# Cross-attention energies on one Trainium2 core: three products in one PSUM bank, scaled in place

## The chip, the cores and the metric

The kernel runs on one core of one Trainium2 chip. The metric is the device time of one execution in microseconds, as the median of several runs. A core has five engines that matter here: TensorE (matrix products into PSUM; its weight loads have a row of their own in the profile, PEld), VectorE (DVE), ScalarE (ACT), GpSimd (POOL) and SyncE (SP), which issues DMAs. PSUM is the memory that TensorE writes: 128 partitions by 8 banks, a bank being 512 float32 values in each partition.

## The reference

There are 32 batches, each with a query input `y` and a key/value input `x` of 256 channels by 1024 positions.

```
x_q = einsum('oc,bcn->bno', w_qk, y)
x_k = einsum('oc,bcn->bon', w_qk, x)
x_v = einsum('oc,bcn->bon', w_v, x) + b_v
energy    = einsum('bnc,bcm->bnm', x_q, x_k)          # 1024 x 1024 a batch
attention = softmax(energy, axis=-1)
attention = attention / (1e-07 + attention.sum(axis=1, keepdims=True))
x_r = einsum('bcn,bnm->bcm', x_v, attention)
x_r = relu(einsum('oc,bcn->bon', w_t, x - x_r) + b_t)
return x + x_r
```

The softmax goes along a row of the energies; the second division goes by the column sums of the softmax.

## The kernel before

**Folding and splitting.** The two query/key weights are folded into one matrix, so the energies are `y` transposed times `G x`. `y` and `G x` are each split into a high part, a low part and a scaled high part (`Split.parts` on ScalarE, then the accumulating DMAs `lower` and `mixed` on GpSimd's queue), and the energies of a block of 128 rows are the sum of three products of such parts, called forms 0, 1 and 2 here. The tiles are `yf` and `gf`. All other large products use a seven-product scheme for 2 x 2 blocks: the class `Seven`, with `Keys` (g, prints as `pg`), `Values` (u, prints as `pu`) and `Attention` (o, prints as `po`). Its methods p1 to p7 are the products, c11 to c22 the combinations. Each uses three PSUM banks, `one`, `two` and `three`: p1, p6, p7 and p4 share `one`, p5 and p3 share `two`, and p2 has `three`.

**Energies.** A batch has 8 blocks `n` of 128 rows. `Energy.products(h)` does one half (512 columns) of a block: six matmuls, forms 0 and 1 into one bank and form 2 into another. `gather(h)` then has ScalarE scale the first bank by `-OVER` into an SBUF tile `es`, and VectorE add the second bank to it, write the result into `e` and take the row minimum (`nm`, carried from half 0 to half 1). `exp` runs on ScalarE over the 1024 columns of `e` in place, with the minimum as its bias, and collects the row sum `rs`. `share` is VectorE's: the reciprocal `ri` of the row sum and `acc += e * ri`, the running column sums. In the loop, `exp` of block n-1 and `share` of block n-2 are issued with block n.

**After the last block** the order of the work is: g.p1, g.p5, `exp(7)`, `share(6)`, g.p2, c11, `share(7)`, g.p6, `columns`, g.p3, c12, g.p7, c22, then the products of `Values` for the next batch, then `inverse` (the reciprocal column sums, `rc`), then the splits for the next batch between the other work, then `Attention`. In `Attention.run` VectorE multiplies `e` by `ri` and `rc` in pieces (`normal`), forms sums of quarters in `et` (`mix`), and TensorE follows with `xpart` and `epart`.

g.p1 and g.p5 are each followed by a ScalarE copy out of PSUM (`gp1s`, `gp5s`), and g.p6 by the copy `gw`; g.p7 accumulates into the bank that `gw` reads.

**Order and buffers.** The wrapper `InOrder` puts the operations of each engine into the order in which the program calls them, so an engine's queue is exactly the order of the source. Every engine operation goes through that wrapper, which is why all of them have line 73 in the profile. PSUM is one pool of eight banks that are handed out in turn: `bank(name)` takes the next one that is free.

The last batch is different: it has no next batch to prepare, and it keeps the unfinished banks of the batch before it (`before`) open while its own energies run.

Of the kernel before, what the change touches and what calls it, by code (L numbers as in the profile page):

```python
# [9 lines left out]
F32 = mybir.dt.float32  # L10
F32R = mybir.dt.float32r
AF = mybir.ActivationFunctionType
ALU = mybir.AluOpType
AX = mybir.AxisListType
# [3 lines left out]
def kernel(  # L18
# [23 lines left out]
    B, C, N = x.shape  # L42
    P = 128
    KC = C // P
    NT = N // P
    MB = 512
    MH = N // MB
# [5 lines left out]
    BIG = 3.0e38  # L53
    UP = 4096.0
    UNDER = 1.0 - 2.0**-13
    OVER = 1.0 + 2.0**-12

    const = ctx.enter_context(tc.tile_pool(name="const", bufs=1))
    xp = ctx.enter_context(tc.tile_pool(name="xp", bufs=2))
    ps_m = ctx.enter_context(tc.tile_pool(name="ps_m", bufs=8, space=bass.MemoryType.PSUM))  # L60

    class InOrder:


        def __init__(self, engine):
            self.engine = engine
            self.last = None
# [9 lines left out]

    pe, dve, act, pool = (InOrder(g) for g in (nc.tensor, nc.vector, nc.scalar, nc.gpsimd))

    def bank(name):  # L80
        return ps_m.tile([P, MB], F32, tag="m", name=name)

    loaded = {}

# [50 lines left out]
    behind = const.tile([P, 1], F32, name="behind")  # L135
    parts = const.tile([P, NB, NG + 1], F32, name="parts")
    dve.memset(parts[:, :, NG], EPS)
    idle = bank("idle")
    for _ in range(5):
        pe.matmul(idle[:, :P], few, few, start=True, stop=True)  # L140
    make_identity(nc, ident)
# [19 lines left out]
        return w, (a11, a12, s4, a22, s1, s2, s3)  # L161


    pg = [bank(f"pg_{i}") for i in range(KC)]
    for i in range(KC):
        for k in range(KC):
            pe.matmul(
# [2 lines left out]
    _, g_left = lefts("g", pg, UP)  # L170

    def turned_weights():

        pt = [bank(f"pt_{i}") for i in range(KC)]
        for i in range(KC):
            for k in range(KC):
                pe.transpose(pt[i][:, ts(k, P)], wt[:, k, ts(i, P)], ident)
        return lefts("wtT", pt)

    def value_weights(wtT):  # L180

        pw = [bank(f"pw_{i}") for i in range(KC)]
        for i in range(KC):
            for k in range(KC):
                pe.matmul(
                    pw[i][:, :C], wv[:, k, ts(i, P)], wtT[:, k, :], start=(k == 0), stop=(k == KC - 1)
                )
        return lefts("wvtT", pw, -1.0)[1]

    def value_bias(wtT):  # L190

        pb = bank("pb")
        for k in range(KC):
            dve.tensor_scalar(bvs[:, k], few, bv[:, k], None, ALU.add)
        for k in range(KC):
            pe.matmul(pb[:, :C], bvs[:, k], wtT[:, k, :], start=(k == 0), stop=(k == KC - 1))
        act.mul(bu.rearrange("p k c -> p (k c)"), pb[:, :C], -1.0)
        act.mul(nbt[:, :, 0], bt[:, :, 0], -1.0)
# [5 lines left out]
    sp = ctx.enter_context(tc.tile_pool(name="sp", bufs=4))  # L204

    def temp(tag, name):
        return cp.tile([P, MB], F32, tag=tag, name=name)
# [67 lines left out]
    class Seven:  # L275
# [3 lines left out]
        def __init__(self, name, b):  # L279
            self.name = name  # L280
            self.b = b

        def bank(self, j):
            return bank(f"p{self.name}{j}_{self.b}")

        def kept(self, p, tag):
            s = temp(tag, f"{self.name}{tag}_{self.b}")
# [107 lines left out]
    class Energy:  # L395
# [3 lines left out]
        def __init__(self, b, n, yf, gf):  # L399
            self.b, self.n = b, n  # L400
            self.yf, self.gf = yf, gf
            self.low = BIG

        def products(self, h):
            self.sums = [bank(f"pe{j}_{self.b}_{self.n}_{h}") for j in range(2)]
            for j in range(3):
                for k in range(KC):
                    pe.matmul(
                        self.sums[j // 2],
                        self.yf[:, j, k, ts(self.n, P)],  # L410
                        self.gf[:, j, k, ts(h, MB)],
                        start=(k == 0 and j != 1),
                        stop=(k == KC - 1 and j != 0),
                    )

        def gather(self, h):


            s = temp(("p1s", "p5s")[h], f"es_{self.b}_{self.n}_{h}")
            act.mul(s, self.sums[0], -OVER)  # L420
            nm = sp.tile([P, 1], F32, tag=f"nm{h}", name=f"nm_{self.b}_{self.n}_{h}")
            dve.tensor_tensor_reduce(
                out=e[:, self.n, ts(h, MB)],
                in0=self.sums[1],
                in1=s,
                scale=1.0,
                scalar=self.low,
                op0=ALU.add,
                op1=ALU.min,
                accum_out=nm,  # L430
            )
            self.low = nm

        def exp(self):
            self.rs = sp.tile([P, 1], F32, tag="rs", name=f"rs_{self.b}_{self.n}")
            row = e[:, self.n, :]
            act.activation(row, row, AF.Exp, bias=self.low, scale=-1.0, accum_out=self.rs)

        def share(self):

# [160 lines left out]
    def columns(b):  # L601

        dve.tensor_reduce(
            parts[:, :, 0],
            acc.rearrange("p (j r) -> p j r", r=G32),
            AX.X,
            ALU.add,
            apply_transpose=True,
        )
# [26 lines left out]
    xr, _ = summed(0)  # L636
    g = Keys(0, xr)
# [26 lines left out]
    u = Values(0, xr)  # L664
# [11 lines left out]
    for b in range(B):  # L676
        more = b + 1 < B
        rows = []

        for n in range(NT):  # L680
            now = Energy(b, n, q.to, g.split.to)
            rows.append(now)
            now.products(0)
            if n == 0:
                e = ep.tile([P, NT, N], F32, tag="e", name=f"e_{b}")
                acc = one.tile([P, N], F32, tag="acc", name=f"acc_{b}")
            now.gather(0)
            now.products(1)
            now.gather(1)
            if n == 0:  # L690
                if b == 0:
                    u.p4()
                    u.c21()
                    xsteps[1]()
                    xsteps[2]()
                elif more:
                    load(b + 1)
                if b == 0:
                    ur, usteps = u.factors()
                    for step in usteps:  # L700
                        step()
                if more and b > 0:
                    xn, xsteps = summed(b + 1)
            if n > 0:
                rows[n - 1].exp()
            if n > 1:
                rows[n - 2].share()
            if more and b > 0 and n in (2, 4, 6):
                xsteps[n // 2 - 1]()

        if more:
            q = Queries(b + 1)
            for i in range(KC):
                q.load(i, nc.sync.dma_start)
            g = Keys(b + 1, xn)
            g.p1()
            g.p5()
            rows[-1].exp()
            rows[-2].share()
            g.p2()  # L720
            g.c11()
            rows[-1].share()
            g.p6()
            columns(b)
            g.p3()
            g.c12()
            g.p7()
            g.c22()
            un = Values(b + 1, xn)
            un.p1()  # L730
            un.p5()
            un.p2()
            un.p6()
        else:
            before.xpart(before.one, 7, True)
            rows[-1].exp()
            rows[-2].share()
            before.epart(before.one, 7)
            ur, usteps = u.factors()
            now = Attention(b, xr, ur)  # L740
            now.begin()
            rows[-1].share()
            columns(b)
            for step in usteps:
                step()
            before.p7s = temp("w", "p7s")
            act.copy(before.p7s, before.one)
        rc = inverse(b)
        if more:
            q.parts(0)  # L750
            q.lower(0)
            un.p3()
            g.p4()
            g.c21()
            un.p7()
            q.parts(1)
            q.lower(1)
            q.mixed(0)
            g.split.parts(0)
            q.mixed(1)  # L760
            g.split.lower(0)

            def between():
                g.split.parts(1)
                g.split.lower(1)
                g.split.mixed(0)
                g.split.mixed(1)

            now = Attention(b, xr, ur)
            now.begin()  # L770
            now.run(un, between=between)
            pool.tensor_copy(behind, now.t4[:, HT - 1, :1])
            if b + 2 < B:
                now.close()
                ur, usteps = un.factors()
                for step in usteps:
                    step()
            else:
                now.epart(now.two, 3, (3,))
                now.c12()  # L780
                now.put()
            before = now
            xr, u = xn, un
        else:
            before.end()
            now.run(None, before)
            now.finish()
# [30 lines left out]
```

## Time and profile before

| | |
|---|---|
| median of 3 runs | 2130.79 us (2130.71 to 2130.84) |
| the profiled execution | 2130.66 us, span 2128.9 us |
| mean granted TensorE clock | 0.994 |
| TensorE busy | 2087.1 us, 98% |
| VectorE busy | 1812.7 us, 85% |
| ScalarE busy | 1179.7 us, 55% |
| GpSimd busy | 681.3 us, 32% |

The span is the time from the first to the last instruction; about 1.8 us of the execution lie around it. Matmuls are pipelined and their ends are modelled, so a busy TensorE is not TensorE at its peak. In the rows, `out<-in` names the tiles that an operation writes and reads (`e<-pe,es` is the operation of `gather` on VectorE), and `x` at the end is a count. A number in brackets is the idle time of the engine before the row, with what released it. A batch in the steady part takes 65.03 us (573.44 to 638.47 us is one). The groups that the change touches:

| operation, before | count | mean |
|---|---|---|
| energy matmul, 128x512 (`pe`) | 3072 | busy 718.7 us in all |
| ScalarE scaling, 128x512 (`es<-pe`) | 512 | 595 ns |
| VectorE add and minimum, half 0 (`e<-pe,es`) | 256 | 686 ns |
| VectorE add and minimum, half 1 (`e<-pe,es,nm`) | 256 | 751 ns |
| VectorE accumulator read (`nm`) | 512 | 83 ns |
| ScalarE exponential, 128x1024 (`e<-e,nm`) | 256 | 1143 ns |
| VectorE `acc`, 128x1024 | 224 | 1294 ns |

### The profile page before, as it was taken

The page shows a single profiled execution, that of the slowest core. Times are in us where ns is not written, and L with a number is a line of the kernel's source. Part 1 is how long each engine was busy: PE and PEld are TensorE (multiplying, and loading weights), DVE is VectorE, ACT ScalarE, POOL GpSimd, SP SyncE. Part 2 cuts the span into 40 slices and gives each one's busy share as a digit, 9 for nine tenths or more (in the row PEclk, how much of TensorE's full clock was granted, in tenths as well). Part 3 has the DMA queues.
Part 4 walks back from the last instruction along what each step waited for, and adds up shares of the span by engine and source line. Part 5 has one row for each costly group of instructions (what it writes and reads, how often), then busy time and mean ns, then how long its engine had stood idle before and what let it go on. Part 6 is the DMA issues. An engine that isn't in the chain of part 4 may idle for free.

```text
span 2128.9 us, 23494 instructions
## 1 busy us (share of the span) xinstructions
PE 2087.1 (98%) x7586; PEld 1290.6 (61%) x7586; DVE 1812.7 (85%) x3024; ACT 1179.7 (55%) x1802; POOL 681.3 (32%) x582
## 2 busy tenths in 40 slices
PE   5999999999999999999999999999999999999998
PEld 4666556665556665566655566655666555666564
DVE  1988889888899888898888998888888889988898
ACT  3664556655556645566555566455665555664562
POOL 2333331333332333323333323333233333233321
PEclk7999999999999999999999999999999999999999
DMA  8456766557766567665577665676655776656740
GB/s 206 88 127 163 177 154 129 139 136 181 168 128 145 129 163 178 155 133 134 136 179 167 128 146 128 163 178 150 135 138 135 177 170 127 148 127 162 178 95 30
DMA packets 108954, 310.34 MB, mean 146 GB/s; under 512 B 10784, under 2 KB 11552, under 8 KB 108832
## 3 DMA queue, kind: packets, MB, share of 16 engines
q0 software_dynamic: 58192, 174.87, 44.9%
q1 hardware_dynamic: 50496, 133.85, 18.5%
q8 instruction: 60, 0.98, 0.2%
q14 instruction: 62, 0.51, 0.1%
q10 hardware_dynamic: 144, 0.13, 0.0%
HBM read 124.78 MB, written 33.55 MB: 74 GB/s over the span
## 4 chain that ended last, share of the span: by engine, by line
PE 61%; DVE 29%; issue 4%; ACT 1%; DMA 1%; DVEq 0%; POOL 0%; ACTq 0%; POOLq 0%
PE pe L73 31%; PE po L73 28%; DVE e L73 14%; DVE acc L73 4%; DVE et L73 4%; DVE gfr L73 3%; DVE rc L73 2%; DVE sc L73 1%; PE pu L73 1%; DVE parts L73 1%; ACT es L73 1%; DVE ri L73 0%; DMA gf<-gfr 0%; PE pg L73 0%; DMA gf<-gf 0%
## 5 line engine op out<-in xcount | busy, mean ns | idle before, releaser
L73 PE MATMUL pe<-gf,yf 128*128 128x512 f32 x3072 | 718.7, 394 | 10.9 <-DMA gf<-gf 10.9
L73 PEld LDWEIGHTS pe<-gf,yf 128*128 128x128 f32 x3072 | 578.0, 188 | 145.7 <-issue 27.3
L73 ACT ACTIVATE es<-pe 128x512 f32<-128x512 f32 x512 | 304.2, 595 | 184.7 <-PE pe L73 184.4
L73 PE MATMUL po<-et,us 128*128 128x512 f32 x768 | 353.9, 597 | 11.5 <-DVE et L73 11.5
L73 DVE SCALAR_TENSOR_TENSOR e<-e,ri,rc 128x512 f32<-128x512 f32 x512 | 347.4, 746 | 1.1
L73 DVE SCALAR_TENSOR_TENSOR acc<-e,ri,acc 128x1024 f32<-128x1024 f32 x224 | 289.9, 1294 | 8.0
L73 ACT ACTIVATE e<-e,nm 128x1024 f32<-128x1024 f32 x256 | 292.7, 1143 | 3.4 <-DVE nm L73 3.3
L73 PEld LDWEIGHTS po<-et,us 128*128 128x128 f32 x768 | 142.9, 190 | 207.0 <-issue 158.4
L73 DVE CUSTOM_DVE_ANT_0 e<-pe,es,nm 128x512 f32<-128x512 f32 x256 | 192.2, 751 | 76.5 <-ACT es L73 49.4
L73 PE MATMUL po<-e,ut 128*128 128x512 f32 x512 | 225.0, 592 | 1.0 <-DVE e L73 1.0
L73 POOL DMA_DIRECT2D yf<-yfr x64 | 55.0, 860 | 533.0 <-ACT yf L73 518.6
L73 DVE CUSTOM_DVE_ANT_0 e<-pe,es 128x512 f32<-128x512 f32 x256 | 175.5, 686 | 51.6 <-ACT es L73 39.1
L73 ACT ACTIVATE z<-po,bt 128x512 f32<-128x512 f32 x31 | 21.4, 689 | 337.1 <-DMA out_dram<-z 234.5
L73 PEld LDWEIGHTS po<-e,ut 128*128 128x128 f32 x512 | 97.2, 190 | 123.8 <-issue 107.4
L73 DVE TENSOR_TENSOR et<-e 128x1024 f32<-128x1024 f32 x128 | 153.7, 1221 | 4.4
L73 POOL TENSOR_TENSOR ut<-ut,bu 128x1024 f32<-128x1024 f32 x64 | 153.5, 2473 | 0.0
L73 POOL DMA_DIRECT2D gf<-gf x64 | 54.8, 856 | 306.3 <-DMA gf<-gfr 262.8
L73 DVE SCALAR_TENSOR_TENSOR z<-z,x 128x512 f32<-128x512 f32 x96 | 132.2, 1377 | 3.3
L73 ACT ACTIVATE yf<-yf 128x1024 fp32r<-128x1024 f32 x128 | 128.2, 1049 | 2.0
L73 ACT ACTIVATE gf<-gf 128x1024 fp32r<-128x1024 f32 x128 | 128.2, 1049 | 2.0
L73 PE MATMUL po<-e,us 128*128 128x512 f32 x256 | 125.3, 592 | 0.0
L73 POOL DMA_DIRECT2D xs<-xs x31 | 37.2, 1201 | 248.4 <-DMA xs<-in_x_dram 240.9
(106 smaller groups left out, 2753.7 us busy)
## 6 DMA issues: line engine op xcount, KB each, us to landing
yfr<-in_ctx_dram SPq DMA_DIRECT2D x64, 512.0 KB, 5.8
yf<-yfr POOLq DMA_DIRECT2D x64, 512.0 KB, 5.1
gf<-gfr POOLq DMA_DIRECT2D x64, 512.0 KB, 10.6
yf<-yf POOLq DMA_DIRECT2D x64, 512.0 KB, 8.0
gf<-gf POOLq DMA_DIRECT2D x64, 512.0 KB, 5.2
out_dram<-z SPq DMA_DIRECT2D x128, 256.0 KB, 3.5
x<-in_x_dram SPq DMA_DIRECT2D x31, 1024.0 KB, 7.4
xs<-in_x_dram SPq DMA_DIRECT2D x62, 512.0 KB, 5.1
```

Of the source, the lines that this page charges most:

```text
L73: self.last = getattr(self.engine, name)(*args, **kwargs)
```

## The change

The two halves of a block now lie in a pair of neighbouring banks, one bank a half. `first()` runs forms 0 and 1 of both halves into the pair, and ScalarE scales the pair in place, 1024 columns in one operation from PSUM to PSUM. `second()` runs form 2 of both halves on top of the scaled values, and VectorE takes one row minimum over the pair. `exp` reads the pair in PSUM and writes `e`. The SBUF tiles `es`, the add on VectorE and the second minimum are gone.

The order is one step deeper: with block n are issued `second` of block n-1, `exp` of block n-2 and `share` of block n-3. What is left over after the last block moves behind it: `exp(6)`, `share(5)` and `second(7)` stand between g.p1 and g.p5.

The banks are no longer handed out in turn. PSUM is one tile of eight banks, and everything has a fixed place: block n of a batch takes pair n mod 4 (n mod 3 in the last batch, banks 0 to 5), g takes banks 2, 0 and 1 as `one`, `two`, `three`, u takes 3, 4, 5, and o takes 6, 7, 0 (7, 4, 5 in the last batch).

```diff
-    ps_m = ctx.enter_context(tc.tile_pool(name="ps_m", bufs=8, space=bass.MemoryType.PSUM))
+    ps_m = ctx.enter_context(tc.tile_pool(name="ps_m", bufs=1, space=bass.MemoryType.PSUM))
...
-    def bank(name):
-        return ps_m.tile([P, MB], F32, tag="m", name=name)
+    banks = ps_m.tile([P, 8, MB], F32, name="banks")
+
+    def bank(j):
+        return banks[:, j]
...
+            last = name == "o" and b == B - 1
+            self.places = {"g": (2, 0, 1), "u": (3, 4, 5), "o": (7, 4, 5) if last else (6, 7, 0)}[name]
 
         def bank(self, j):
-            return bank(f"p{self.name}{j}_{self.b}")
+            return bank(self.places[(1, 5, 2).index(j)])
...
-            self.low = BIG
-
-        def products(self, h):
-            self.sums = [bank(f"pe{j}_{self.b}_{self.n}_{h}") for j in range(2)]
-            for j in range(3):
-                for k in range(KC):
-                    pe.matmul(
-                        self.sums[j // 2],
-                        self.yf[:, j, k, ts(self.n, P)],
-                        self.gf[:, j, k, ts(h, MB)],
-                        start=(k == 0 and j != 1),
-                        stop=(k == KC - 1 and j != 0),
-                    )
-
-        def gather(self, h):
...
+            at = 2 * (n % (4 if b + 1 < B else 3))
+            self.pair = banks[:, at : at + 2]
+
+        def products(self, forms):
+            for h in range(MH):
+                for j in forms:
+                    for k in range(KC):
+                        pe.matmul(
+                            self.pair[:, h],
+                            self.yf[:, j, k, ts(self.n, P)],
+                            self.gf[:, j, k, ts(h, MB)],
+                            start=(j == 0 and k == 0),
+                            stop=(j == 2 and k == KC - 1),
+                            skip_group_check=True,
+                        )
+
+        def first(self):
+
+            self.products((0, 1))
+            act.mul(self.pair, self.pair, -OVER)
+
+        def second(self):
+
+            self.products((2,))
+            self.low = sp.tile([P, 1], F32, tag="nm", name=f"nm_{self.b}_{self.n}")
+            dve.tensor_reduce(self.low, self.pair.rearrange("p h m -> p (h m)"), AX.X, ALU.min)
 
         def exp(self):
             self.rs = sp.tile([P, 1], F32, tag="rs", name=f"rs_{self.b}_{self.n}")
-            row = e[:, self.n, :]
-            act.activation(row, row, AF.Exp, bias=self.low, scale=-1.0, accum_out=self.rs)
+            act.activation(
+                e[:, self.n, :],
+                self.pair.rearrange("p h m -> p (h m)"),
+                AF.Exp,
+                bias=self.low,
+                scale=-1.0,
+                accum_out=self.rs,
+            )
...
-            now.products(0)
+            now.first()
...
-            now.gather(0)
-            now.products(1)
-            now.gather(1)
+            if n > 0:
+                rows[n - 1].second()
...
-            if n > 0:
-                rows[n - 1].exp()
             if n > 1:
-                rows[n - 2].share()
+                rows[n - 2].exp()
+            if n > 2:
+                rows[n - 3].share()
...
             g = Keys(b + 1, xn)
             g.p1()
+            rows[-2].exp()
+            rows[-3].share()
+            rows[-1].second()
             g.p5()
             rows[-1].exp()
             rows[-2].share()
...
         else:
+            rows[-2].exp()
+            rows[-3].share()
+            rows[-1].second()
             before.xpart(before.one, 7, True)
             rows[-1].exp()
             rows[-2].share()
```

More of the change, by code (lines that the diff above doesn't have):

```diff
@@ L137 @@
     dve.memset(parts[:, :, NG], EPS)
-    idle = bank("idle")
+    idle = bank(7)
     for _ in range(5):
@@ L161, in lefts @@
         return w, (a11, a12, s4, a22, s1, s2, s3)
-    pg = [bank(f"pg_{i}") for i in range(KC)]
+    pg = [bank(i) for i in range(KC)]
     for i in range(KC):
@@ L172, in turned_weights @@
     def turned_weights():
-        pt = [bank(f"pt_{i}") for i in range(KC)]
+        pt = [bank(6 + i) for i in range(KC)]
         for i in range(KC):
@@ L180, in value_weights @@
     def value_weights(wtT):
-        pw = [bank(f"pw_{i}") for i in range(KC)]
+        pw = [bank(4 + i) for i in range(KC)]
         for i in range(KC):
@@ L190, in value_bias @@
     def value_bias(wtT):
-        pb = bank("pb")
+        pb = bank(6)
         for k in range(KC):
@@ L416, in gather @@
-        def gather(self, h):
[L419 to L432, printed above, removed]
+            at = 2 * (n % (4 if b + 1 < B else 3))
```

## The prediction

> **What bounds the kernel now.** I read the page first, then the chain of waits from 568 to 640 us (one whole batch in the steady part), then the timelines of the engines there. The page says that TensorE is nearly always busy and that the chain is shared:
>
> ```profile
> PE 2087.1 (98%) x7586; PEld 1290.6 (61%) x7586; DVE 1812.7 (85%) x3024; ACT 1179.7 (55%) x1802; POOL 681.3 (32%) x582
> ...
> PE 61%; DVE 29%; issue 4%; ACT 1%; DMA 1%; DVEq 0%; POOL 0%; ACTq 0%; POOLq 0%
> ```
>
> In one batch the chain runs on TensorE through attention and energies, crosses to VectorE near the last energies, and comes back after the normalisation:
>
> ```profile
> 573.44 21.36 PE pe L73 x94
> ...
> 595.52 0.68 DVE e L73
> ...
> 600.64 1.30 DVE acc L73
> ...
> 607.50 6.73 DVE e L73 x10
> ...
> 616.90 1.24 DVE et L73
> 618.13 0.04 issue
> 618.18 2.84 PE po L73 x6
> ```
>
> So a batch (65.03 us from 573.44 to 638.47) is decided in two places: when VectorE gets through its queue, and when TensorE gets to the products that use `et`. The weight loads show how near TensorE is at the second place (gap of an unhindered load: 0.24):
>
> ```profile
> 616.83 0.19 PEld L73 LDWEIGHTS po<-et,us 128*128 128x128 f32 x1 [0.24 <-issue]
> 618.18 0.30 PEld L73 LDWEIGHTS po<-et,us 128*128 128x128 f32 x2 [1.16 <-DVE et L73]
> ...
> 619.57 0.19 PEld L73 LDWEIGHTS po<-xs,wtTs 128*128 128x128 f32 x1 [0.24 <-issue]
> ```
>
> Loads come 0.43 apart, so five after 616.83 would be at 618.98; it is 619.57. TensorE has only 0.59 us to spare in the whole stretch. Any TensorE delay between the energies and 616 beyond 0.59 lengthens the batch. That is what I look for.
>
> **Durations.** ScalarE's timeline gives the blocks' pace and the end of the energies:
>
> ```profile
> 591.07 0.59 ACT L73 ACTIVATE es<-pe 128x512 f32<-128x512 f32 x1
> ...
> 593.79 0.59 ACT L73 ACTIVATE es<-pe 128x512 f32<-128x512 f32 x1
> 594.88 0.60 ACT L73 ACTIVATE es<-pe 128x512 f32<-128x512 f32 x1 [0.50 <-PE pe L73]
> ...
> 597.47 1.15 ACT L73 ACTIVATE e<-e,nm 128x1024 f32<-128x1024 f32 x1
> ...
> 598.71 0.59 ACT L73 COPY gw<-pg 128x512 f32<-128x512 f32 x1
> ```
>
> One block is 2.72 us of TensorE, 0.2267 a matmul. The first `pg` matmul is at 595.08; the matmul before the `es` of 594.88 is two from the end and ends at 594.63, so a reader starts 0.25 after its matmul. VectorE meanwhile needs 2.94 a block (its pairs of `e<-pe,es` start at 586.70, 589.64, 592.58, 595.52): it is the slower one and falls 0.86 behind.
>
> **Part 1, VectorE per block.** Removed: the two `e<-pe,es` with their accumulator reads, 1.55 us (586.70 to the reciprocal at 588.25). Added: one minimum over 1024 elements of PSUM, which the trace does not have. Rows: a 512-wide TENSOR_TENSOR from PSUM is 0.68 and the next starts 0.60 after it; 512 more elements cost 0.54 (SBUF TENSOR_TENSOR 1.22 at 1024, 0.68 at 512). So 1.22 to its result, 1.14 to the next start. Bounds: small TENSOR_REDUCE rows (32x160 in 0.307, 32x32 in 0.175 to 0.203) give 0.81 to 1.03 ns an element, 1.01 us at the least; twice the 512 row is 1.36. I take 1.14, by the nearest row in source and width. With the share (reciprocal and `acc`, 597.06 to 598.45: 1.39) a block needs 2.53, less than TensorE's 2.72: VectorE keeps up and its backlog goes. Who is late next? The order.
>
> **Part 2, the end of the energies.** Everything is one block deeper: after TensorE's last block there now wait `share(4)`, `share(5)`, the last reduction, `share(6)`, c11, `share(7)`, where before there were `share(5)`, `share(6)`, c11, `share(7)`. TensorE finishes all but the last four energy matmuls at 595.08 - 0.91 = 594.17. Then VectorE: reduction 6 from 594.42, `share(4)` from 595.56, `share(5)` from 596.95, reduction 7 from 598.34, result 599.56. The last exponential starts at 599.62; before, 597.47: 2.15 later. ScalarE's queue is in order, and behind that exponential stands the copy `gw` that g.p7 on TensorE needs (1.24 after the exponential, load another 0.63 later, from 598.71 and 599.34). So g.p7 moves from 599.34 to 601.49, and all of TensorE's work behind it, x parts and epart(one, 1) too: +2.15. Less the spare 0.59: **+1.56 a batch**. VectorE's own way is shorter: `share(6)` 599.48, c11 600.87, `share(7)` 601.47 against 600.45, +1.02, so `et` is there at 619.15 when TensorE arrives at 619.41.
>
> The other moved steps have cover. `second(7)` stands behind g.p1 on TensorE, with its four matmuls (0.91) ahead of g.p5; its result is in PSUM by 597.9, and VectorE is not free for it before 598.34. `exp(6)` stands on ScalarE behind `gp1s` and is done by 598.7; `share(6)` asks for it at 599.48. `exp(7)` ends, with its accumulator, at 600.86; `share(7)` asks at 601.47.
>
> A second wait lies under the first one. g.p1 now writes bank 2, which exponential 5 reads. Forms 0 and 1 of the last block end at 593.27, their scaling (0.595 plus 0.43 for 512 more: 1.02) starts at 593.52, the exponential at 594.45, done 595.6: TensorE waits there from 593.94 to 595.64, 1.7 us, with the last energies queued behind. Alone it would bring g.p7 to 600.64, +1.30, or +0.71 a batch. It holds even if the reduction were free.
>
> **Part 3, at no cost.** Scaling 128x1024 in PSUM: bounds 0.98 (512 row plus 0.38) to 1.19 (two rows); with the exponential (1.24 to the next start) about 2.2 us of ScalarE a block, under 2.72, covered by TensorE's 2.72; above it, each 0.1 us costs 0.8 a batch. The exponential from PSUM: 0.69 for 512 with a bias plus 0.43, 1.12, like the 1.14 now; bounds 1.05 to 1.38. TensorE's 12 matmuls a block stay 12. ScalarE's splits and GpSimd's DMAs for the next batch slip by 2.15 while the energies slip by 1.56; the third form is first needed in `second(0)`, 2.7 us later than now, which covers it. SP's loads wait for nothing new.
>
> **Part 4, the two ends.** First batch: TensorE waits for the third form's DMAs:
>
> ```profile
> 41.55 0.77 PE L73 MATMUL pe<-gf,yf 128*128 128x512 f32 x1 [4.49 <-DMA gf<-gf]
> 47.76 3.32 PE L73 MATMUL pe<-gf,yf 128*128 128x512 f32 x7 [5.44 <-DMA gf<-gf]
> ```
>
> Forms 0 and 1 of block 1 and the product u.p4 can now go ahead of that wait, 12 matmuls and 8 small ones, so the energies end 4.0 us earlier (67.8 for 71.8). The deeper tail, with the first three `acc` at 1.8 to 2.5 us as they are there now, lets reduction 7 end at 74.1 and g.p7 start at 76.0 instead of 78.34; with the spare there (0.98 by the loads) **-3.3**, between -6 and 0. Last batch: three pairs, so a block waits for the exponential three before it, which stands behind the newest scaling: 1.81 for eight matmuls, 0.25 to wake ScalarE, 0.93 and 1.14 there, 0.2 to wake TensorE, 4.33 a block from block 3 on, not 2.72. Counted from the first energy matmul: block 3 begins at 8.9, block 7 at 26.2; reduction 6 at 29.15, reduction 7 at 33.1 behind two shares, its exponential until 35.7, `share(7)` until 37.2, and 0.8 for the slow last `acc` (2.10) that is there now too. `columns` starts at 38.0 instead of 30.1 (2060.1 to 2090.22): **+7.9**, bounds 5 and 10.
>
> **Sum.** The profiled execution is 2130.66 (span 2128.9 and 1.8 around it), 0.13 under the median. 30 batches x 1.56 = 46.8; 2130.66 + 46.8 - 3.3 + 7.9 = 2182. With the reduction between 1.01 and 1.36 and some tenths of wake-up time, +1.1 to +2.2 a batch: 33 to 66. Ends: 2130.7 + 33 - 6 + 5 = 2163 and 2130.7 + 66 + 0 + 10 = 2207.
>
> The new pauses of TensorE (1.7 and 0.7 us a batch) raise one question. Behind the pauses of 4.49 and 5.44 us in the first batch, the seven matmuls of the row above take 0.47 us each, twice the usual; behind the 0.9 us wait at 618.18 they do not slow down. For 1.7 us no row of before decides, and I take the nearer one, no slowing. [...]
>
> **Rivals.** (a) Faster: VectorE's backlog is all that matters. Its place is 595.52, where it is 0.86 behind; taken away in 31 batches, with the ends, 2130.7 - 26.7 + 7.9 = 2112. For it: the chain does pass there, and VectorE loses 0.41 a block. Against: it decides only if the last exponential starts before 598.06 (597.47 + 0.59) and g.p1 does not wait, which needs a reduction of 0.36 us, under every row. 5%. (b) Pauses slow TensorE: seven matmuls at 0.47 instead of 0.23 are 1.7 us, once a batch: 2182 + 51 = 2233. 6%. (c) ScalarE becomes the bound: if operations in PSUM cost a quarter more than my rows, 2.72 is passed; at 2.9 a block 31 x 8 x 0.18 = 45 more, 2227. 4%. (d) The change does not do what it says: `banks` is one tile, and if waits are made for the whole tile instead of for banks, scaling and reductions stop TensorE in every block, about 2 us x 256 = 500, 2640. 2%. (e) The waits cancel, within 4 us of now. 3%.
>
> **How the numbers follow.** The forecast gets 80%. A difference under 0.2% (4.3 us) can't be told from no change. Faster: (a) and a little of the rest, 0.06. Same: 0.03. Slower: forecast, (b), (c), (d), 0.91. The range is the forecast's 2163 to 2207, widened slightly for wake-up times I can't see: 2158 to 2208.
>
> **What would show it.** Right: in the chain, `gw` or the last exponential between VectorE and `pg`; a TensorE wait of about 1.7 us at the first `pg` load and another before g.p7; no `et` wait at the later products; reductions of 1.2 us; a batch of 66.6 us; 4.3 us between blocks in the last batch. Wrong: a steady batch under 65 us, blocks further apart than 2.72 in the middle, or matmuls of 0.47 after the pauses.

## The result, and the profile after the change

The changed kernel takes 2182.99 us (median of 5 runs, 2182.50 to 2184.16) against 2130.71 us (median of 5 runs now, three of them those of the table above): a ratio of 1.0247, 95% interval 1.0232 to 1.0262. The forecast was 2182, slower. The profiled execution is 2182.99 us with a span of 2181.2, 52.3 more than before.

The page of the changed kernel, shares of the engines and of the chain:

```profile
PE 2097.1 (96%) x7586; PEld 1291.8 (59%) x7586; DVE 1764.8 (81%) x2256; ACT 1155.4 (53%) x1546; POOL 682.2 (31%) x582
...
PE 86%; DVE 9%; ACT 3%; DMA 1%; issue 1%; DVEq 0%; ACTq 0%; POOLq 0%
```

VectorE and ScalarE have less to do than before (VectorE by 48 us), and the kernel is slower all the same. VectorE's share of the chain fell from 29% to 9%: it no longer carries the path through the normalisation, but only one short stretch a batch. The chain of waits shows that stretch (in all rows after the change, every PSUM tile is called `banks`):

```profile
604.77 1.22 DVE nm L73
...
606.10 1.29 DVE acc L73
...
607.50 1.28 DVE acc L73
608.78 1.14 DVE nm L73
...
610.01 1.21 ACT e L73 x2
611.22 0.48 ACT gw L73
611.70 0.04 issue
611.74 59.41 PE banks L73 x222
```

Reduction 6, two shares, reduction 7, the last exponential, the copy `gw`, and then TensorE for 59.41 us until the same place in the next batch. TensorE's weight loads show both waits at the end of the energies (an unhindered load has 0.24 in the brackets):

```profile
606.03 0.30 PEld L73 LDWEIGHTS banks<-x,g 128*128 128x128 f32 x2 [1.79 <-ACT e L73]
...
611.74 0.30 PEld L73 LDWEIGHTS banks<-xs,gs 128*128 128x128 f32 x2 [1.06 <-ACT gw L73]
...
629.66 0.19 PEld L73 LDWEIGHTS banks<-et,us 128*128 128x128 f32 x1 [0.24 <-DVE et L73]
```

The first is g.p1 at its bank, the second g.p7 behind `gw`. The third is the fifth of the eight loads of `et`, the one that waited 1.16 us before: TensorE now comes too late to wait there. From one `gw` to the next a batch takes 66.50 us, before 65.03.

### The profile page after: what moved, and what is told of

It reads as the page before. It is cut to its first block, busy times and chain, and to the rows that moved or that the text cites. A ratio compares the mean times of both kernels' runs of the same rounds, so it can differ in the third digit from the quotient of the medians.

```text
span 2181.2 us, 21835 instructions
## 1 busy us (share of the span) xinstructions
PE 2097.1 (96%) x7586; PEld 1291.8 (59%) x7586; DVE 1764.8 (81%) x2256; ACT 1155.4 (53%) x1546; POOL 682.2 (31%) x582
## 4 chain that ended last, share of the span: by engine, by line
PE 86%; DVE 9%; ACT 3%; DMA 1%; issue 1%; DVEq 0%; ACTq 0%; POOLq 0%
PE banks L73 86%; DVE acc L73 4%; DVE nm L73 4%; ACT e L73 2%; ACT gw L73 1%; DMA gf<-gf 0%; DVE ri L73 0%; DVE e L73 0%; DMA gf<-gfr 0%; ACT banks L73 0%; ACT yf L73 0%; ACT gf L73 0%; DVE et L73 0%; DVE parts L73 0%; DVE rc L73 0%
## 5 line engine op out<-in xcount | busy, mean ns | idle before, releaser
L73 PE MATMUL banks<-gf,yf 128*128 128x512 f32 x3072 | 740.4, 400 | 13.0 <-ACT e L73 6.7
L73 PEld LDWEIGHTS banks<-gf,yf 128*128 128x128 f32 x3072 | 578.8, 189 | 163.5 <-issue 37.3
L73 DVE TENSOR_REDUCE nm<-banks 128x1 f32<-128x1024 f32 x256 | 313.1, 1223 | 213.8 <-PE banks L73 204.2
L73 ACT ACTIVATE banks<-banks 128x1024 f32<-128x1024 f32 x256 | 258.1, 1008 | 223.7 <-PE banks L73 223.6
L73 PE MATMUL banks<-et,us 128*128 128x512 f32 x768 | 345.6, 592 | 0.8 <-DVE et L73 0.8
L73 ACT ACTIVATE e<-banks,nm 128x1024 f32<-128x1024 f32 x256 | 284.7, 1112 | 20.0 <-DVE ri L73 16.4
L73 PEld LDWEIGHTS banks<-et,us 128*128 128x128 f32 x768 | 145.8, 190 | 185.1 <-issue 176.1
L73 PE MATMUL banks<-e,ut 128*128 128x512 f32 x512 | 225.0, 592 | 1.6 <-DVE e L73 1.6
L73 PE MATMUL banks<-e,us 128*128 128x512 f32 x256 | 125.3, 592 | 0.0
L73 PE MATMUL banks<-et,ut 128*128 128x512 f32 x256 | 115.1, 592 | 0.0
```

What stands on the lines that cost most here:

```text
L73: self.last = getattr(self.engine, name)(*args, **kwargs)
```

## The experiments

The batch times in this section go from one `gw` copy to the next on ScalarE's timeline. Each experiment's ratio is to the kernel before, run again beside it (2130.37 us for e1 to e4, 2131.14 us for e5 to e8). The last two columns say where two steps stand in a steady batch (the one that runs at 600 us), counted from its first energy matmul: the weight load of g.p7 on TensorE, and the start of `share(7)` on VectorE.

| kernel | median, us | ratio to the kernel before (95%) | a batch in the steady part, us | g.p7 | `share(7)` |
|---|---|---|---|---|---|
| before | 2130.71 | 1 | 65.03 | 26.46 | 27.57 |
| changed | 2182.99 | 1.0247 (1.0232 to 1.0262) | 66.50 | 28.54 | 28.62 |
| e1: g in other banks | 2190.83 | 1.0284 (1.0270 to 1.0298) | 66.50, five of 68.1 to 68.4 | 28.53 | 28.61 |
| e2: `gw` ahead of the last exponential | 2187.28 | 1.0267 (1.0253 to 1.0281) | 66.63 | 28.08 | 29.16 |
| e3: both | 2168.57 | 1.0179 (1.0165 to 1.0193) | 66.04 | 26.48 | 28.60 |
| e4: last batch, exponential first | 2175.18 | 1.0210 (1.0196 to 1.0224) | 66.47 | 28.50 | 28.58 |
| e5: another order throughout | 2116.90 | 0.9933 (0.9920 to 0.9945) | 64.67 | 27.51, behind u.p1 | 26.61 |
| e6: e5 without the filled wait | 2128.59 | 0.9989 (0.9980 to 0.9998) | 65.03 | 27.08 | 26.62 |
| e7: e1 with the wait filled | 2170.62 | 1.0184 (1.0170 to 1.0198) | 66.07 | 28.53, behind u.p1 | 28.61 |
| e8: kernel before, one share later | 2166.63 | 1.0165 (1.0151 to 1.0179) | 66.20 | 26.46 | 28.74 |

### e1 to e3: which of the waits decides

e1 gives g banks that are free early; e2 changes ScalarE's order; e3 does both.

```diff
-            self.places = {"g": (2, 0, 1), "u": (3, 4, 5), "o": (7, 4, 5) if last else (6, 7, 0)}[name]
+            self.places = {"g": (0, 1, 2), "u": (3, 4, 5), "o": (7, 4, 5) if last else (6, 7, 1)}[name]
```

> Only the fixed places of g and o change (g: banks 0, 1, 2 instead of 2, 0, 1; o: 6, 7, 1 instead of 6, 7, 0), so g.p1 no longer writes a bank that exponential 5 reads. Theory (the order on ScalarE: g.p7 waits for gw behind the last exponential behind reduction 7): the 1.8 us wait at the first g load goes, but g.p7 stays where it is, about 28.5 us after the first energy matmul of its batch, because reduction 7 waits for VectorE's shares and not for TensorE; 2183 us, within 4. Rival (the bank wait is what costs): the batch loses 0.7 us, 30 x 0.7 = 21, 2162 us.

```diff
             g.p5()
-            rows[-1].exp()
             rows[-2].share()
             g.p2()
             g.c11()
-            rows[-1].share()
             g.p6()
+            rows[-1].exp()
+            rows[-1].share()
             columns(b)
```

> Only the place of the last exponential changes: ScalarE takes gw (after g.p6) first and exponential 7 behind it. Theory: gw then waits for g.p6 on TensorE, which the bank wait still holds until about 610.5 on the clock of the changed kernel's batch, so g.p7 comes only 0.4 us earlier; exponential 7 moves 1.2 us later and share(7) 0.7 us later; VectorE becomes what ends last, 1.75 us behind the kernel before, a batch of 66.8 us, 30 x 0.3 = 9 us more than the changed kernel: 2192 us. Rival (only the TensorE wait at g.p7 counts): 30 x 0.4 = 11 us less, 2172 us.

> Both edits together: g in banks 0, 1, 2 and gw ahead of the last exponential. Theory: TensorE goes through g without a wait, and what is left is VectorE's deeper queue, 1.05 us a batch behind the kernel before; the wait for et at the later products comes back. Batch 66.1 us, 30 x 0.4 = 12 us under the changed kernel: 2171 us. Rival (the two TensorE waits are the whole cost): a batch of 65.0 us as before, 2183 - 44 = 2139 us. Rival (the bank wait is what costs): no more than from the bank change alone.

Measured: in e1 the wait at the first g load is gone, g.p7 stays where it was (28.53 us, the theory's 28.5), and a batch is still 66.50 us. So the bank wait costs nothing as long as `gw` comes late: the rival of 2162 us falls. But the time was 2190.8, 4 us above the theory's bound. Five slower batches make that up: together they lose 8.45 us, and the profiled execution of 2191.1 us would be 2182.7 without it. What slowed them is taken up under e7.

In e2 g.p7 comes 0.46 us earlier and the batch is longer, 66.63 us, because the last exponential now holds up `share(7)` by 0.54 us; the chain crosses to VectorE there and returns to TensorE at `et`, as it did in the kernel before. The theory had a batch of 66.8 and 9 us more than the changed kernel, the rival under 66.2 and 11 us less; measured are 4.3 us more.

In e3 g.p7 is back at 26.48, `share(7)` is still at 28.60, and the batch is 66.04 us, the theory's 66.1. The weight loads of e3 show the old wait again, longer than before the change:

```profile
624.84 0.30 PEld L73 LDWEIGHTS banks<-et,us 128*128 128x128 f32 x2 [1.36 <-DVE et L73]
```

So without TensorE's two waits, VectorE's deeper queue alone costs 1.0 us a batch. TensorE's waits and VectorE's queue are two paths of nearly one length, and taking one away leaves the other.

### e4: the last batch

```diff
+            if not more and n > 1:
+                rows[n - 2].exp()
             now.first()
...
-            if n > 1:
+            if more and n > 1:
                 rows[n - 2].exp()
```

> Only the last batch changes: ScalarE takes exponential n-2 ahead of the scaling of block n, not behind it. Theory (with three pairs, a block waits for the exponential three before it, which stands behind the newest scaling): blocks come 2.7 to 2.9 us apart instead of 4.38, five blocks x 1.5 = 7 to 8 us less, 2175 us. Rival (the last batch loses its 8 us in the deeper tail, whatever the pairs): 0 to 2 us less.

Measured: 2175.2 us, 7.8 less than the changed kernel; the steady batches are the same to 0.03 us. TensorE's timeline of the last batch, first in the changed kernel (two of five such blocks), then in e4:

```profile
2117.55 3.02 PE L73 MATMUL banks<-gf,yf 128*128 128x512 f32 x12 [1.35 <-ACT e L73]
2121.93 3.04 PE L73 MATMUL banks<-gf,yf 128*128 128x512 f32 x12 [1.36 <-ACT e L73]
```

```profile
2104.59 22.08 PE L73 MATMUL banks<-gf,yf 128*128 128x512 f32 x92
```

The blocks came 4.38 us apart with three pairs of banks, and come with no gap in the row once the exponential that frees a pair does not stand behind a scaling that has time. Three pairs are enough; the queue order was the price.

### e7: what slowed e1

TensorE reaches g.p7 earlier in e1 and then waits for `gw` in one piece (2.68 us idle between weight loads). In five of its batches (the expectation below counts six) the products behind that wait are slower. TensorE's timeline of e1, the product u.p1 in a batch of 66.5 us, and the same place in one of 68.4, with the pause ahead of it:

```profile
613.62 1.05 PE L73 MATMUL banks<-wvtT,x 128*128 128x128 f32 x8
```

```profile
1412.69 1.12 PE L73 MATMUL banks<-xs,gs 128*128 128x512 f32 x2 [1.86 <-ACT gw L73]
1413.65 1.57 PE L73 MATMUL banks<-wvtT,x 128*128 128x128 f32 x8
1415.02 1.91 PE L73 MATMUL banks<-wvtTs,xs 128*128 128x128 f32 x8
```

The granted clock from 1411 to 1416 is 0.80, against 1.00 in the 4 us before. The copy `uw`, which follows u.p6, starts 6.98 to 7.02 us after `gw` in each of the five slow batches and 5.36 or 5.37 us after it in the others from the third on. To tell the pause from the places of the banks, e7 keeps the places and puts u.p1 into the pause:

```diff
             g.c12()
+            un = Values(b + 1, xn)
+            un.p1()
             g.p7()
             g.c22()
-            un = Values(b + 1, xn)
-            un.p1()
             un.p5()
```

> The bank change of e1 and u.p1 ahead of g.p7, nothing else. Theory (e1's six batches of 68.1 us come from a lower TensorE clock after the pause before g.p7, which is 2 us long there): the pause is 1.1 us, no batch is slowed, TensorE's delay falls under VectorE's, and the batch is VectorE's 66.1 us: 2171 us. Rival (those batches are slowed by the places of the banks): several batches stay 1.6 us longer than the others.

Measured: 2170.6 us, batches of 66.07 us, and from the third on none over 66.4. In e1's rows the pause is 1.85 us idle at 612.66, and the next product starts 0.90 after u.p1 (613.62 to 614.52), so an estimate of what is left of the pause here is 0.95. `uw` starts 4.46 or 4.47 us after `gw` from the third batch on; in the second, of 67.25 us, it is 6.11. The places, kept from e1, are not the cause: with the pause shortened, no later batch is slowed.

### e8: depth alone, in the kernel before

```diff
-            if n > 1:
-                rows[n - 2].share()
+            if n > 2:
+                rows[n - 3].share()
...
+            rows[-3].share()
             g.p1()
             g.p5()
```

The same line stands ahead of the last batch's tail.

> The kernel before, with its two banks a half and its SBUF scaling, where only share is one block later (share(n-3) in the loop, one more share behind the last block). Theory (depth of the order costs, not the place of the energies): VectorE ends its shares 1.2 us later, the exponentials and TensorE's g products stay where they are, a batch of 66.2 us: 30 x 1.2 = 36 us over the kernel before, 2166 us. Rival (VectorE has room for it among the energies, since the sum of its work is the same): 2130 us.

Measured: 2166.6 us, 66.20 us a batch. One share moved behind the last block moves `share(7)` by 1.17 us and costs 1.17 us a batch with the old banks, the old scaling and the old reductions, while g.p7 stays at 26.46. The energies' place in PSUM is not needed for VectorE's part of the loss; TensorE's part, by which the changed kernel loses 0.3 us more, is not in e8.

### e5 and e6: the same operations in another order

```diff
         for n in range(NT):
...
+            if n > 1:
+                rows[n - 2].exp()
             now.first()
...
-            if n > 1:
-                rows[n - 2].exp()
-            if n > 2:
-                rows[n - 3].share()
+            if n > 1:
+                rows[n - 2].share()
...
             g.p1()
             rows[-2].exp()
-            rows[-3].share()
             rows[-1].second()
             g.p5()
             rows[-1].exp()
             rows[-2].share()
             g.p2()
-            g.c11()
-            rows[-1].share()
             g.p6()
+            rows[-1].share()
             columns(b)
+            g.c11()
             g.p3()
             g.c12()
-            g.p7()
-            g.c22()
             un = Values(b + 1, xn)
             un.p1()
+            g.p7()
+            g.c22()
             un.p5()
```

The last batch's tail loses its `share(5)` too, which the loop has done.

> The changed kernel with four edits of order: exponential n-2 goes to ScalarE ahead of the scaling of block n (in every batch); share(n-2) follows in the same pass of the loop, so one share fewer is left at the end; c11 stands behind columns; and u.p1 stands ahead of g.p7 on TensorE. Theory: g.p1 finds its bank free, reduction 7 comes 1.4 us earlier, TensorE fills its wait for gw with u.p1, VectorE reaches the normalisation 0.5 us earlier than in the kernel before: a batch of 64.5 us, the last batch without its 1.5 us waits; 2130 - 30 x 0.5 - 2 = 2113 us, between 2108 and 2122. Rival (energies kept in PSUM cost time of their own, whatever the order): no better than the kernel before, 2130 us or more.

> The kernel of e5 without its last edit: g.p7 stands ahead of u.p1 again. Theory: TensorE waits 0.65 us for gw, less the 0.59 us spare, so TensorE and not VectorE sets the batch, 65.1 us: 30 x 0.6 = 18 us over e5, about 2131 us. Rival (VectorE's queue alone sets the batch): the same as e5.

Measured: e5 takes 2116.9 us, 0.7% under the kernel before and 3% under the changed one. The theory's 64.5 us a batch is 64.67. The energies in PSUM are kept, so the rival falls: whatever price they have of their own is smaller than what the order gains. Whether they have one stays open, because the kernel before was not run with u.p1 in the wait and c11 behind `columns`. e5's page and the second wait on `et`:

```profile
PE 2085.0 (99%) x7586; PEld 1288.1 (61%) x7586; DVE 1772.3 (84%) x2256; ACT 1154.7 (55%) x1546; POOL 680.9 (32%) x582
...
PE 96%; DVE 2%; DMA 1%; issue 1%; ACT 1%; DVEq 0%; POOLq 0%
```

```profile
613.97 0.30 PEld L73 LDWEIGHTS banks<-et,us 128*128 128x128 f32 x2 [0.64 <-DVE et L73]
```

e6, with g.p7 back ahead of u.p1, takes 2128.6 us and 65.03 us a batch. The theory said 65.1 and 2131 and the rival the same as e5, so the one wait for `gw` (1.01 in the brackets of its load) is worth 0.36 us a batch even here, and TensorE decides. The other three edits of e5 were run only together.

The two columns of the table now give the batches. Take the delay of `share(7)` against the kernel before, and the delay of g.p7 less the 0.61 us that the changed kernel did not lose of it (2.08 less 1.47); add the larger one to 65.03. That makes 66.49, 66.62, 66.06, 65.04 and 66.20 us for e1, e2, e3, e6 and e8, each within 0.02 us of the measured one. (In e5 and e7 u.p1 stands ahead of g.p7, so their loads can't be compared so.)

## Why the prediction was right, point by point

**The reduction.** Taken at 1.22 us to its result and 1.14 to the next start; the changed kernel's 256 reductions have a median of 1.224, and `ri` follows 1.14 after. A row of the same source and half the width, with the slope of another operation, was enough.

**VectorE keeps up, and the backlog goes.** Before it needed 2.94 us a block; now reductions follow at 2.72 (596.61, 599.33, 602.05, 604.77), TensorE's pace. Right, and worth nothing by itself, as the working said.

**+1.56 a batch by TensorE.** It was 1.47. The lines, first of the kernel before, then of the changed one (its g.p7 load at 611.74 is shown above):

```profile
572.88 22.36 PE L73 MATMUL pe<-gf,yf 128*128 128x512 f32 x96
...
599.34 0.30 PEld L73 LDWEIGHTS pg<-xs,gs 128*128 128x128 f32 x2 [0.65 <-ACT gw L73]
```

```profile
583.20 21.46 PE L73 MATMUL banks<-gf,yf 128*128 128x512 f32 x92
```

From the first energy matmul of its batch to the load of g.p7 are 28.54 us (583.20 to 611.74), before 26.46 (572.88 to 599.34): 2.08 later, where I had 2.15. The last exponential starts 2.22 later instead of 2.15, but from PSUM it takes 1.11 us, not 1.14, and `gw` starts 1.11 after it instead of 1.24. The spare was 0.61 instead of 0.59. e3 agrees that this path set the time: with g.p7 back at its old place the batch falls to 66.04.

**+1.02 by VectorE.** `share(7)` starts 28.62 after the first energy matmul, before 27.57: 1.05, and e3 makes it the bound with 66.04 - 65.03 = 1.01.

**The wait under the wait.** Predicted at 1.7 us, it is 1.79 in the brackets, less 0.24. That it holds nothing up while `gw` is late is e1. The prediction said it would hold "even if the reduction were free"; that was not run.

**The last batch, +7.9.** From the first energy matmul to `columns` are 38.6 us (2104.00 to 2142.62), before 30.4 (2059.79 to 2090.22; the prediction had read 2060.1 for the first of these): 8.2 more. Its blocks come 4.38 apart, predicted 4.33; the 0.2 taken to wake TensorE, which no row of before shows, is 0.14 after the change (the exponential ends at 2121.79, the products start at 2121.93). e4 takes 7.8 us back by the order alone.

**The first batch, -3.3: wrong.** The row of energies ends at 67.9, as predicted, but g.p7 starts at 79.86, not 76.0, 1.5 later than before instead of 2.3 earlier; 0.8 of it is a later start of the energies (36.14 for 35.39). The failed step is "the first three `acc` at 1.8 to 2.5 us as they are there now". First the kernel before, then the changed one, each with GpSimd's first two adds:

```profile
56.35 5.11 POOL L73 TENSOR_TENSOR ut<-ut,bu 128x1024 f32<-128x1024 f32 x2
...
59.50 2.52 DVE L73 TENSOR_SCALAR acc<-e,ri 128x1024 f32<-128x1024 f32 x1
...
63.67 1.96 DVE L73 SCALAR_TENSOR_TENSOR acc<-e,ri,acc 128x1024 f32<-128x1024 f32 x1
...
67.29 1.84 DVE L73 SCALAR_TENSOR_TENSOR acc<-e,ri,acc 128x1024 f32<-128x1024 f32 x1
```

```profile
56.53 5.11 POOL L73 TENSOR_TENSOR ut<-ut,bu 128x1024 f32<-128x1024 f32 x2
...
58.48 3.72 DVE L73 TENSOR_SCALAR acc<-e,ri 128x1024 f32<-128x1024 f32 x1
...
63.44 2.37 DVE L73 SCALAR_TENSOR_TENSOR acc<-e,ri,acc 128x1024 f32<-128x1024 f32 x1
...
67.04 2.23 DVE L73 SCALAR_TENSOR_TENSOR acc<-e,ri,acc 128x1024 f32<-128x1024 f32 x1
...
71.70 2.08 PE L73 MATMUL banks<-x,g 128*128 128x512 f32 x2 [3.79 <-ACT e L73]
```

The three took 2.0 us more, because they start earlier and end where they did before: at 62.20, 65.81 and 69.27 for 62.02, 65.63 and 69.13, with GpSimd's adds 0.18 us later too. So their durations could not be carried over; the ends could. Exponential 5 came late by that, and g.p1 waited 3.79 us for its bank, the wait that the prediction had counted in the steady batches alone. The granted clock was 0.50 from 70.8, inside that pause, to 77.5, and the products ran at half pace (2.08 us for a pair that takes 1.02); the prediction had taken no slowing.

**The sum.** The first batch gave +0.5 instead of -3.3 (counted where its later products stand, 99.90 for 99.39), from there to the last batch's first energy matmul are 43.7 us more instead of 46.8, the last batch 8.2 instead of 7.9, and what follows 0.1 less. Two errors of 3 and 4 us cancel; that the total of 52.3 comes so near to 51.4 is luck.

**The rivals.** (a) needed a last exponential by 598.06 and fell with the chain. (b), slower TensorE after pauses, did not happen in steady batches of the changed kernel, where the granted clock is 1.00 from 77.7 us to 2177.2, the end of TensorE's work. It did happen in its first batch (0.50 from 70.8 to 77.5), and in five batches of e1, where the pause was one long one: the rival was near. (c) ScalarE scales a pair in 1.01 us and has 0.60 to spare a block. (d) Waits are made for the banks, not for the tile: TensorE runs 92 of a batch's 96 energy matmuls in one row of 21.46 us (583.20) without a gap.

## What to carry to other kernels

When an engine falls behind in a loop, making its work cheaper helps only if the last piece still leaves the loop as early as before. Count what stands behind the last block on each queue, in order, and add the slack of the next engine: here one more block of depth (1.0 to 1.2 us of VectorE a batch, 2.1 of TensorE) outweighed 0.41 us saved on each of eight blocks. In this kernel the depth could be taken back by order alone (e5): an operation that frees a buffer goes ahead of one that has time, and a wait that stays is filled with work that is ready. In the first batch, where VectorE works beside GpSimd's adds, the ends of its operations carried over to the changed kernel and their durations did not: a duration taken from such a place is worth a second look.

## What the runs showed of the hardware that was not expected

Behind a TensorE pause of under 2 us the products ran slower in some batches and not in others. In e1 TensorE's row is idle ahead of g.p7 for 1.85 us at 612.66 and at 1344.57, and for 1.86 at 1412.69. Behind the first of these pauses u.p1 and the product after it take 1.05 and 1.06 us, behind the other two 1.70 and 1.92, and 1.57 and 1.91. The granted clock is 0.86 from 1338 to 1350 and 0.80 from 1411 to 1416; from 1270 to 1282, where no product is slowed, it is 1.00. By the time from `gw` to `uw` (6.98 to 7.02 us against 5.36 or 5.37) the batch behind the 3.16 us idle at the end of the first one is slowed, and four in a row from 1343.94 to 1616.71; the five lose 1.6 to 1.9 us. In the changed kernel, with pauses of 1.4 and 0.2 idle, `uw` follows `gw` after 5.36 to 5.38 us in every batch from the second on; its one longer batch after the first (66.76) has a granted clock of 1.00, and why it is longer is open. Why one pause of 1.85 us is followed by slower products and another is not, and why four slowed batches follow each other, is not shown by these runs.

VectorE's first `acc` took several times its length beside GpSimd's adds. It (fp32, 128x1024) takes 0.75 us in a steady batch of the changed kernel (at 595.22) and 3.72 in the first one; in the kernel before 2.52 in the first. There it starts 3.15 us after the first of those adds, in the changed kernel 1.95, and in both it ends 5.67 us after it, 0.56 us behind the second add's end. That the adds hold it is inferred from this; no run moves them.
